# FFN fused values stored as interleaved high and low words: the down products read every second word as weights

## The chip, the cores and the metric

The kernel runs on one core of a Trainium2 chip. The metric is the device time of one execution in microseconds (us), taken as the median of several runs; lower is better. Every time below comes from those runs or from one profiled execution of the kernel.

## The reference

The input x has shape (4, 512, 512) in float32. Two blocks follow each other, each on a layer-normed input and each added back to it:

```python
# attention: 16 heads of 32
q, kv = (x @ W_q.T), (x @ W_kv.T)          # per head of 32
qf, kvf = fft(q), fft(kv)                  # each scaled to unit length over the head
qv = qf * cumsum(kvf, axis=1)              # running sum over the 512 positions
x = x + real(ifft(qv)) @ W_o.T             # (on layernorm(x))

# feed-forward (FFN), weights rounded to float8_e4m3fn first
gate = silu((x @ gate_w) * gate_scale)     # 512 -> 1536
up = (x @ up_w) * up_scale
fuse = gate * up
x = x + (fuse @ down_w) * down_scale       # 1536 -> 512 (on layernorm(x))
```

## The kernel before

The four batch entries have 512 positions each, in four chunks of 128. The kernel writes its instructions in an order fixed by hand; no scheduler moves them. Tiles come from pools: a tile with a `tag` takes the oldest of that tag's `bufs` buffers, and its first writer waits for the last user of what lay there.

The attention runs over the 16 chunks. For every chunk the running sum is a product of a triangle of ones (`tri_r`) with the key `kn`. The key is split into two tiles, `kh` (its value rounded to float32r by ScalarE) and `kl` (what is left, by VectorE). `running` multiplies both with `tri_r` and adds them up; here the halves are the moving operand. `k_scaled` takes one buffer of tag "kh" and one of tag "kl", each with three buffers.

The FFN runs over 48 steps, that is four batches (`b`) by twelve groups of 128 of the 1536 hidden values (`m`), with n = 12 b + m. Step n is `inner(n)`:

- 16 products of 512 columns (L525): `gu` for gate and for up, each over four blocks of the 512 inputs and over the high and low halves `yh`, `yl` of the normed input. The FFN weights `wg`, `wu` are here the stationary operand (lhsT, loaded into TensorE by LDWEIGHTS); the halves are the moving one.
- ScalarE's silu gives `g` (L536), VectorE multiplies into `f` (L538), ScalarE casts the high half `fh` (L546), VectorE subtracts to get the low half `fl` (L548). These two halves of one [128, 512] value again go into tags "kh" and "kl", the buffers of the attention's halves. For one step, n == STEPS - LATE = 44, they take two buffers of tag "qv".

`down(n)` then multiplies the halves with the down weights `wd`. Here the halves are the weights that TensorE loads: 128 of their 512 columns for each of the four chunks c, eight products for a step (L561):

```python
for c in cs:
    for v in fused[n]:                       # fh, then fl
        nc.tensor.matmul(
            pds[b][c][:, s],
            lhsT=v[:, c * P : (c + 1) * P],  # loaded as weights
            rhs=wd[:, m, s],                 # streamed
```

`down(n - 1)` stands behind `inner(n)` in the order of TensorE, so that the halves of step n - 1 are made while the 16 products of step n run. The quantisation of the later FFN weights still runs on VectorE and ScalarE during the first steps (`next_parts`). The last four steps (`LATE`) keep their down products for the end: they run chunk by chunk there, chunk 3 in two halves of 256 columns, so that the results of the first chunks leave while the last are computed. `scaled_out` (L575) and `added_out` (L579) finish a chunk and write it out.

Of the kernel before, what the change touches and what calls it, by code (L numbers as in the profile page):

```python
# [9 lines left out]
F32R = mybir.dt.float32r  # L10
# [5 lines left out]
P = 128  # L16
# [19 lines left out]
def tile_fft_attention_then_fp8_ffn(  # L36
# [39 lines left out]
    B, S, D = x.shape  # L76
# [10 lines left out]
    work = ctx.enter_context(tc.tile_pool(name="work", bufs=2))  # L87
# [242 lines left out]
    def nm(i):  # L330
        return "%d_%d" % chunks[i]
# [49 lines left out]
    def scaled(i, j, t):  # L381
        nc.vector.scalar_tensor_tensor(
            heads(t),
            heads(pqs[i][j]),
            st_x[i][1],
            rns[i, j].unsqueeze(2).to_broadcast([P, H, HD]),
            ALU.mult,
            ALU.mult,
        )

    def k_scaled(i):
        kn = work.tile([P, D], F32, tag="kn", name=f"kn_{nm(i)}", bufs=1)
        scaled(i, 1, kn)
        if i in carries:
            row = carries.pop(i)
            nc.vector.tensor_tensor(kn[:1, :], kn[:1, :], row, ALU.add)  # L396
        kh = work.tile([P, D], F32R, tag="kh", name=f"kh_{nm(i)}", bufs=3)
        kl = work.tile([P, D], F32R, tag="kl", name=f"kl_{nm(i)}", bufs=3)
        nc.scalar.copy(kh, kn)
        kns[i] = (kn, kh, kl)  # L400

# [78 lines left out]
    def y_mean(b, c):  # L480
        st_y[b, c] = mean(ys[b][:, c, :], f"f{b}_{c}")
# [36 lines left out]
    def inner(n, on_pe, on_act, between):  # L518
        b, m = divmod(n, MC)
        pgu = []  # L520
        for j, w in enumerate((wg, wu)):
            p = ps.tile([P, S], F32, tag="b", name=f"gu{j}_{b}_{m}")
            for k in range(KC):
                for v in (yhs[b], yls[b]):
                    nc.tensor.matmul(  # L525
                        p,
                        lhsT=w[:, k, m * P : (m + 1) * P],
                        rhs=v[:, k, :],
                        start=k == 0 and v is yhs[b],
                        stop=k == KC - 1 and v is yls[b],  # L530
                    )
            pgu.append(p)
            if j == 0:
                on_pe(n, 0)
        g = work.tile([P, S], F32, tag="tmp", name=f"g_{b}_{m}")
        nc.scalar.activation(g, pgu[0], AF.Silu, scale=gus[:, 0, m : m + 1])  # L536
        f = work.tile([P, S], F32, tag="qn", name=f"f_{b}_{m}")
        nc.vector.scalar_tensor_tensor(f, pgu[1], gus[:, 1, m : m + 1], g, ALU.mult, ALU.mult)  # L538
        on_act(n)
        if n == STEPS - LATE:  # L540
            fh = work.tile([P, S], F32R, tag="qv", name=f"fh_{b}_{m}")
            fl = work.tile([P, S], F32R, tag="qv", name=f"fl_{b}_{m}")
        else:
            fh = work.tile([P, S], F32R, tag="kh", name=f"fh_{b}_{m}", bufs=3)
            fl = work.tile([P, S], F32R, tag="kl", name=f"fl_{b}_{m}", bufs=3)
        nc.scalar.copy(fh, f)  # L546
        between(n)
        nc.vector.tensor_tensor(fl, f, fh.bitcast(F32), ALU.subtract)  # L548
        fused[n] = (fh, fl)
        on_pe(n, 1)  # L550
# [78 lines left out]
    summed(0, 0)  # L629
    norms(0, 0)  # L630
    k_scaled(0)
    k_low(0)

# [21 lines left out]
    x_mean(3)  # L655
    summed(1, 0)
    k_scaled(1)
    norms(1, 0)
    fold_out(wo, raw[2], 0)
# [33 lines left out]
    for i in range(3, N):  # L693
# [3 lines left out]
        if 0 <= i - (N - 9) < TC:  # L697
            load_y(0, [i - (N - 9)])
        spectrum(i, 1)
        k_scaled(i - 1)  # L700
        at(finish, i - 4)
        while wanted:
# [50 lines left out]
    def on_pe(n, part):  # L753
        if part == 1 and n == 0:
            running(N - 1)
            products(N - 1)
            combined(N - 1)
            v_out(N - 1)
            project(N - 3, "tp")
            load_unit(U1 + 2)  # L760
            load_unit(U1 + 3)
            v_back(N - 1)

    def on_act(n):
        b, m = divmod(n, MC)
        if b + 1 < B and 0 <= m - 3 < TC:
            y_mean(b + 1, m - 3)

    def between(n):
        if 0 < n < MC:  # L770
            next_parts(3 if n < 4 else 1)
# [30 lines left out]
    for n in range(STEPS):  # L802
        inner(n, on_pe, on_act, between)
        if 0 < n <= STEPS - LATE:
            b, m = divmod(n - 1, MC)
            down(n - 1, range(TC))
            if m == MC - 1:
                for c in range(TC):
                    scaled_out(b, c)
                    added_out(b, c, nc.gpsimd)  # L810
        behind(n)
# [3 lines left out]
    b = B - 1  # L815
# [83 lines left out]
```

## Time and profile before

| | |
|---|---|
| median of 3 runs | 460.06 us (459.68 to 460.41) |
| the profiled execution, whole | 460.13 us |
| its span in the profile | 458.3 us |
| mean granted clock of TensorE | 0.999 |
| PE (TensorE matmul) busy | 451.8 us, 1680 products |
| PEld (TensorE weight load) busy | 309.4 us, 1680 loads |
| DVE (VectorE) busy | 282.8 us |
| ACT (ScalarE) busy | 212.7 us |
| POOL (GpSimd) busy | 189.9 us |

The span is the stretch that the profiler sees; the 1.8 us between it and the whole time lie around it. PEld runs beside PE: the load of the next weights overlaps the product that runs. The duration of a record is not its share of time on TensorE, since products and loads are pipelined: 512-column products have records of 389 ns but start 227 ns after each other. The engines' names in the profile's rows are followed by the line of the kernel and by the tiles (output<-inputs); numbers of buffers are left out.

### The profile page before, as it was taken

Reading aid. Unit: us, or ns where it says so; the run is one execution under the profiler, and the core shown is the slowest. Engines: PE = TensorE matmul, PEld = TensorE weight load, DVE = VectorE, ACT = ScalarE, POOL = GpSimd, SP = SyncE. Lnnn points to the kernel's source line nnn. Section 1 sums busy time; section 2 is a strip of 40 time slices with the busy share of each in tenths; the row PEclk is TensorE's granted clock in tenths of the full one; section 3 lists DMA queues with packets and bytes.
Section 4 is the critical chain, followed back from the end, with each engine's and each line's share of the span. In section 5 each row is a group of like instructions: output and inputs, shape, how many; then the busy total and the mean of one; then the engine's idle time right before and its main releaser. Section 6 shows DMA issues by size and latency. Waiting matters only on the chain.

```text
span 458.3 us, 5074 instructions
## 1 busy us (share of the span) xinstructions
PE 451.8 (99%) x1680; PEld 309.4 (68%) x1680; DVE 282.8 (62%) x393; ACT 212.7 (46%) x430; POOL 189.9 (41%) x133
## 2 busy tenths in 40 slices
PE   9999999999999999999999999999999999999995
PEld 8544444444444445676888888888888888888884
DVE  1376999997999889798995432343533333532235
ACT  4468665556875632338934225433235432222220
POOL 0477897898897778510342230022401021400001
PEclk9999999999999999999999999999999999999999
DMA  8826356656678665752341050430131420200002
GB/s 301 296 78 190 99 162 161 183 148 186 196 205 210 172 142 162 206 156 81 92 93 23 0 185 23 93 69 1 48 138 39 98 48 1 92 1 0 0 1 92
DMA packets 91753, 51.22 MB, mean 112 GB/s; under 512 B 70608, under 2 KB 71248, under 8 KB 91728
## 3 DMA queue, kind: packets, MB, share of 16 engines
q1 hardware_dynamic: 91056, 50.75, 39.0%
q8 instruction: 13, 0.21, 0.2%
q10 hardware_dynamic: 672, 0.16, 0.2%
q14 instruction: 12, 0.10, 0.1%
HBM read 34.09 MB, written 16.78 MB: 111 GB/s over the span
## 4 chain that ended last, share of the span: by engine, by line
PE 82%; DVE 5%; ACT 4%; POOL 4%; issue 3%; DMA 2%; SPq 1%; DVEq 0%; ACTq 0%; POOLq 0%
PE gu L525 37%; PE pd L561 19%; PE pq L358 14%; PE po L457 7%; POOL rn L379 2%; DMA qv_all<-qv 1%; PE cum L413 1%; PE pkv L162 1%; ACT sq L369 1%; PE pw L162 1%; PE idle L592 1%; ACT qm L218 1%; DVE kn L396 1%; PE pwo L175 1%; ACT qa L217 1%
## 5 line engine op out<-in xcount | busy, mean ns | idle before, releaser
L379 POOL TENSOR_TENSOR rn<-ss,nhalf 128x16 f32<-128x16 f32 x32 | 103.6, 3237 | 12.6 <-DVE ss L374 12.4
L538 DVE SCALAR_TENSOR_TENSOR f<-gu,gus,g 128x512 f32<-128x512 f32 x48 | 36.0, 749 | 105.3 <-PE gu L525 101.7
L525 PE MATMUL gu<-yh,wg 128*128 128x512 f32 x192 | 76.6, 399 | 0.0
L561 PE MATMUL pd<-wd,fh 128*128 128x512 f32 (+1 forms) x196 | 75.1, 385 | 0.0
L561 PE MATMUL pd<-wd,fl 128*128 128x512 f32 (+1 forms) x196 | 75.0, 385 | 0.0
L525 PE MATMUL gu<-yh,wu 128*128 128x512 f32 x192 | 74.8, 390 | 0.0
L525 PE MATMUL gu<-yl,wg 128*128 128x512 f32 x192 | 74.7, 389 | 0.0
L525 PE MATMUL gu<-yl,wu 128*128 128x512 f32 x192 | 74.7, 389 | 0.0
L546 ACT CAST fh<-f 128x512 fp32r<-128x512 f32 x48 | 29.8, 621 | 81.9 <-DVE f L538 81.9
L536 ACT ACTIVATE g<-gu,gus 128x512 f32<-128x512 f32 x48 | 32.9, 686 | 53.3 <-PE gu L525 53.0
L358 PE MATMUL pq<-wq,xT 128*128 128x512 f32 x128 | 57.6, 593 | 0.0
L358 PE MATMUL pq<-wkv,xT 128*128 128x512 f32 x128 | 57.5, 592 | 0.0
L457 PE MATMUL po<-wo,qvT 128*128 128x512 f32 x128 | 57.5, 592 | 0.0
L548 DVE TENSOR_TENSOR fl<-f,fh 128x512 fp32r<-128x512 f32 x48 | 35.7, 744 | 27.5 <-ACT fh L546 27.5
L579 POOL TENSOR_TENSOR o<-o,ys 128x512 f32<-128x512 f32 x13 | 16.4, 1294 | 79.0 <-DVE o L575 70.1
L358 PEld LDWEIGHTS pq<-wkv,xT 128*128 128x128 f32 x128 | 24.2, 190 | 30.1 <-issue 28.5
L297 POOL TENSOR_TENSOR dev_f<-dev_f,nhalf 128x1 f32<-128x1 f32 x16 | 12.3, 768 | 72.9 <-ACT dev_f L296 72.7
L525 PEld LDWEIGHTS gu<-yh,wg 128*128 128x128 f32 x192 | 36.0, 188 | 8.9 <-issue 0.7
L561 PEld LDWEIGHTS pd<-wd,fh 128*128 128x128 f32 x196 | 36.8, 188 | 7.4
L561 PEld LDWEIGHTS pd<-wd,fl 128*128 128x128 f32 x196 | 36.8, 188 | 7.4
L358 PEld LDWEIGHTS pq<-wq,xT 128*128 128x128 f32 x128 | 23.2, 190 | 27.4 <-issue 27.0
L525 PEld LDWEIGHTS gu<-yl,wg 128*128 128x128 f32 x192 | 36.0, 188 | 8.2 <-issue 1.0
(88 smaller groups left out, 612.1 us busy)
## 6 DMA issues: line engine op xcount, KB each, us to landing
x<-in_x SPq DMA_DIRECT2D x16, 256.0 KB, 3.4
xT<-in_xT SPq DMA_DIRECT2D x16, 256.0 KB, 3.1
qv_all<-qv SPq DMA_DIRECT2D x16, 256.0 KB, 4.1
zv<-qv_all SPq DMA_DIRECT2D x64, 64.0 KB, 2.6
y_all<-x SPq DMA_DIRECT2D x16, 256.0 KB, 2.8
ys<-y_all SPq DMA_DIRECT2D x16, 256.0 KB, 3.8
xn_all<-xn_f SPq DMA_DIRECT2D x16, 256.0 KB, 2.5
z<-xn_all SPq DMA_DIRECT2D x64, 64.0 KB, 2.6
```

What stands on the lines that cost most here:

```text
L162: nc.tensor.matmul(pw[:, j * P : (j + 1) * P], lhsT=r[:, j, i * P : (i + 1) * P], rhs=fwd, start=True, stop=True,)
L297: nc.gpsimd.tensor_tensor(rstd, rstd, nhalf[:, 0:1], ALU.pow)
L358: nc.tensor.matmul(pq, lhsT=xTs[i][:, k, :], rhs=w[:, k, :], start=k == 0, stop=k == KC - 1)
L379: nc.gpsimd.tensor_tensor(rns[i, j], sss.pop((i, j)), nhalf, ALU.pow)
L457: nc.tensor.matmul(po, lhsT=qvT[:, k, :], rhs=wo[:, k, :], start=k == 0, stop=k == KC - 1)
L525: nc.tensor.matmul(p, lhsT=w[:, k, m * P : (m + 1) * P], rhs=v[:, k, :], start=k == 0 and v is yhs[b], stop=k == KC - 1 and v is yls[b],)
L536: nc.scalar.activation(g, pgu[0], AF.Silu, scale=gus[:, 0, m : m + 1])
L538: nc.vector.scalar_tensor_tensor(f, pgu[1], gus[:, 1, m : m + 1], g, ALU.mult, ALU.mult)
L546: nc.scalar.copy(fh, f)
L548: nc.vector.tensor_tensor(fl, f, fh.bitcast(F32), ALU.subtract)
L561: nc.tensor.matmul(pds[b][c][:, s], lhsT=v[:, c * P : (c + 1) * P], rhs=wd[:, m, s], start=m == 0 and v is fused[n][0], stop=m == MC - 1 a ...
L579: add.tensor_tensor(o, o, ys[b][:, c, s], ALU.add)
```

## The change

The two halves of a split value become one tile. For the attention's key it is `k2`, [128, 2, 512], with the high half in front and the low half behind it; each half is still contiguous. For the FFN's fused value it is `f2`, [128, 512, 2]: word 2j is the high half and word 2j + 1 the low half of value j. `fh` and `fl` become views of it with a step of two words. ScalarE's cast writes with this step, VectorE's subtraction reads and writes with it, and every load of weights for a down product reads 128 words with it. Both tiles use one tag, "kk", of three buffers, each as large as a "kh" and a "kl" buffer together. Step 44's tile takes a buffer of the tag "qa", which the quantisation has left by then.

```diff
@@ k_scaled
-        kh = work.tile([P, D], F32R, tag="kh", name=f"kh_{nm(i)}", bufs=3)
-        kl = work.tile([P, D], F32R, tag="kl", name=f"kl_{nm(i)}", bufs=3)
+        k2 = work.tile([P, 2, D], F32R, tag="kk", name=f"k2_{nm(i)}", bufs=3)
+        kh, kl = k2[:, 0, :], k2[:, 1, :]
@@ inner
         if n == STEPS - LATE:
-            fh = work.tile([P, S], F32R, tag="qv", name=f"fh_{b}_{m}")
-            fl = work.tile([P, S], F32R, tag="qv", name=f"fl_{b}_{m}")
+            f2 = work.tile([P, S, 2], F32R, tag="qa", name=f"f2_{b}_{m}")
         else:
-            fh = work.tile([P, S], F32R, tag="kh", name=f"fh_{b}_{m}", bufs=3)
-            fl = work.tile([P, S], F32R, tag="kl", name=f"fl_{b}_{m}", bufs=3)
+            f2 = work.tile([P, S, 2], F32R, tag="kk", name=f"f2_{b}_{m}", bufs=3)
+        fh, fl = f2[:, :, 0], f2[:, :, 1]
```

No instruction is added, removed or moved: on each engine the built program has the same instructions in the same order with the same waits. What differs is the addresses and the step of the operands named above.

## Prediction

> **What bounds the kernel now.** I read the chain of waits first, because it says which engine an added nanosecond has to be on. From about 184 us on it is TensorE alone, step after step, without a gap: 16 gate and up products, then eight down products.
>
> ```profile
> PE 82%; DVE 5%; ACT 4%; POOL 4%; issue 3%; DMA 2%; SPq 1%; DVEq 0%; ACTq 0%; POOLq 0%
> ```
>
> The same chain in order of time, near its end (start, length, engine, line, how many):
>
> ```profile
> 424.37 3.63 PE gu L525 x16
> 427.99 1.81 PE pd L561 x8
> 429.81 3.63 PE gu L525 x16
> 433.43 1.81 PE pd L561 x8
> 435.25 10.88 PE gu L525 x48
> 446.13 7.36 PE pd L561 x40
> ```
>
> The reader is to see that the FFN's time is a count of products times their beat: 1.81/8 and 3.63/16 are both 227 ns, whether the weights are `fh`/`fl` or `wg`/`wu`. So whatever the changed loads do matters only if it lengthens this beat, or starves TensorE of its halves.
>
> The groups of instructions, kept apart by shape, give the loads and the two engines that write the halves:
>
> ```profile
> L561 PEld LDWEIGHTS pd<-wd,fh 128*128 128x128 f32 x196 | 36.8, 188 | 7.4
> L561 PEld LDWEIGHTS pd<-wd,fl 128*128 128x128 f32 x196 | 36.8, 188 | 7.4
> L548 DVE TENSOR_TENSOR fl<-f,fh 128x512 fp32r<-128x512 f32 x48 | 35.7, 744 | 27.5 <-ACT fh L546 27.5
> L546 ACT CAST fh<-f 128x512 fp32r<-128x512 f32 x48 | 29.8, 621 | 81.9 <-DVE f L538 81.9
> L346 PEld LDWEIGHTS row<-tab,less 128*128 128x128 f32 x16 | 2.2, 137 | 3.8 <-issue 2.9 <-ACT wo L176 0.7 <-ACT kh L399 0.2
> ```
>
> 392 loads change, 188 ns each; ACT and DVE sit idle for tens of us before their part. The last row is a load whose 128 columns are one and the same word (step 0): 137 ns. It is a transpose as well, so it shows only weakly that the time of a load hangs on its step.
>
> The timeline of the end shows what a load costs when it does not fit behind a wide product. Columns: start, length, engine, instruction.
>
> ```profile
> 447.67 0.69 DVE L548 TENSOR_TENSOR fl<-f,fh 128x512 fp32r<-128x512 f32 x1 [0.69 <-ACT fh L546]
> ...
> 448.69 0.19 PEld L561 LDWEIGHTS pd<-wd,fl 128*128 128x128 f32 x1
> ...
> 452.00 0.28 PE L561 MATMUL pd<-wd,fl 128*128 128x256 f32 x1
> 452.00 0.19 PEld L561 LDWEIGHTS pd<-wd,fh 128*128 128x128 f32 x1
> 452.12 0.28 PE L561 MATMUL pd<-wd,fh 128*128 128x256 f32 x1
> 452.12 0.19 PEld L561 LDWEIGHTS pd<-wd,fl 128*128 128x128 f32 x1
> ```
>
> Products of 256 columns start 120 ns apart, each with a load of its own. So a contiguous load holds the load path for at most 120 of its 188 ns; the rest is latency that overlaps. At full width 227 - 120 = 107 ns of each beat are free for a slower load. In the 16 half-width products at the very end (2 halves x 4 steps x 2) nothing is known to be free. Early in the span the 128-column products are closer together still:
>
> ```profile
> 9.56 0.99 PEld L162 LDWEIGHTS pw<-tab,raw 128*128 128x128 f32 x8
> ```
>
> Eight loads in 0.99 us, 0.19 the last one: (0.99 - 0.19)/7 = 114 ns a load. I take 114 ns as what a contiguous load holds; it is a bound from above.
>
> **The loads.** 392 loads read 128 words spread over 256. No row of the trace has a load with step two. Below: no cost, or a gain (rival three). [...] The nearest rows are steps 0 and 1, 137 and 188 ns: 51 ns more for one more step, so a third step would be 239 ns, or 114 + 51 = 165 ns held. Holding in proportion to the words spanned gives 2 x 114 = 228 ns. I take the doubling: the step-0 row is a transpose and its slope is weak, and the words spanned are what the tile doubles. Then
> - 376 full-width products: 228 against a beat of 227, hidden: 0 us within the rounding. Were the true hold 120 ns, it would be 376 x (240 - 227) = 4.9 us.
> - 16 half-width products: 16 x (228 - 120) = 1.7 us, all on the path, for the last `scaled_out` halves start only when the last product ends (DVE was 0.29 us idle for it). With 165 ns held it would be 0.7 us.
>
> [...]
>
> **The halves' writers.** ScalarE's cast (621 ns) and VectorE's subtraction (median 691 ns) now write with step two. Below: nothing, as the FFT's strided pieces on VectorE (240 elements in runs of 15 with gaps) take 402 ns where a contiguous 128x256 product takes 421. Above: as if all 1024 words were passed, for which the rows are 1048 ns on ACT (L217) and 1330 ns on DVE (L254): +0.43 and +0.64 us. The runs of those FFT pieces are long, mine have one word, so I take half: +0.21 and +0.32 us. In most steps this is covered: `fl` ends at 430.23 (429.54 + 0.69) and is first loaded after 433 us, about 3 us later. The cover is thin in two places. In step 1 VectorE is late with quantisation; `fl` ends at 197.44 and its load starts at 197.54: 0.32 - 0.10 = 0.22 us of stall. At the end `fl` of the last step ends at 448.36 and is loaded at 448.69: 0.21 + 0.32 - 0.33 = 0.20 us. Together 0.4 us; from 0 to (0.64 - 0.10) + (1.07 - 0.33) = 1.3 us.
>
> [...]
>
> **What is shared now.** `k2` and the tag "kk" join buffers that were released apart: a new writer waits for the later of two readers, but the low half's reader directly follows the high half's on TensorE, and every wait in the built program is the one it was. Queues, transfers and quantisation are not touched. 0 us. Step 44's buffer of tag "qa" was last read by quantisation at 242 us (L254), some 190 us before.
>
> **The sum.** 1.7 + 0.4 = +2.1 us. The profiled execution took 460.13 us (span 458.3, 1.8 around it), 0.07 above the median of 460.06, so it stands for the runs: 462.2 us.
>
> **Rivals.**
> 1. Nothing happens: the load reads step two as fast as step one and the writers do too. For it: idle time before both writers and 107 free ns a beat. Against it: 16 half-width beats and two thin places where small extras show. 460.1 us, up to 460.9 if only the writers slow down.
> 2. The loads set the beat at full width. It decides from 227 ns held, twice my 114, so the forecast stands at its edge. At 2.5 times (285 ns): 376 x 58 + 16 x 165 ns = 24.4 us, 485 us with the writers' 0.4. At four times (456 ns): 376 x 229 + 16 x 336 ns = 91 us, 552 us. For it: the load is the only thing that every product does, and I cannot bound it from above. Against it: a factor over 2 means that skipping a word costs more than reading it.
> 3. Faster. float32 products (two passes, L358) start 429 ns apart, 214.5 for a pass of 512 columns; float32r ones 227. Something of 12 ns goes on in each float32r product, and if it is the handover from a load, a load that reads differently could save it: 392 x 12 ns = 4.7 us, 455.4 us. It needs the 12 ns to hang on the load's addresses; against it, `gu` with other weights has the same 227.
> That the change does not do what it says is excluded: the built program's weight operands have a step of two.
>
> **How the numbers follow.** Forecast (loads stretched, but hidden at full width): 0.38, from 460.9 to 466 (4.9 + 16 x 120 ns, or less, without the writers' extremes). Rival 1: 0.29. Rival 2: 0.26, half of it below 485. Rival 3: 0.07. About 0.2% (0.9 us) is what a measurement of this kernel can tell from no change: faster 0.07, same 0.29, slower 0.38 + 0.26 = 0.64. The range goes from 459.5, the low side of rival 1, to 484, half of rival 2; some 0.13 above and 0.06 below are left out. By the forecast's own case alone it would be 460.9 to 466.
>
> **What would show it.** Right: full-width down products still 227 ns apart (1.81 us for eight), the half-width ones some 228 instead of 120, `fl` and `fh` between 1 and 2 times as long, waits of TensorE for `fl` once near 197 us and once near 448 us. Wrong: eight down products in more than 1.9 us (rival 2), half-width ones still at 120 ns (rival 1), fewer than 1.8 us (rival 3).

## The result, and the profile after

The changed kernel takes 462.91 us (461.93 to 463.89, 4 runs) against 460.04 us before: 1.0059 times as long, with a 95% interval of 1.0045 to 1.0073, or +2.9 us (2.1 to 3.4). The profiled execution of after is its shortest run, 461.93 us, with a span of 460.1.

The chain of waits after the change, in order of time (start, length, engine, line, how many), at the same place as before:

```profile
424.02 1.87 PE pd L561 x8
425.89 3.63 PE gu L525 x16
429.52 1.87 PE pd L561 x8
431.39 3.63 PE gu L525 x16
435.02 1.87 PE pd L561 x8
436.89 10.89 PE gu L525 x48
447.78 7.53 PE pd L561 x40
```

Eight down products take 1.87 us instead of 1.81, and the forty at the end 7.53 instead of 7.36. Gate and up products stand nearly as before, 3.63 us for sixteen. Start to start in the trace, a full-width down product (512 columns) takes 233.4 ns instead of 226.7. That is 6.7 ns x 376 = 2.5 us, spread evenly over the FFN. By the starts in the trace the sixteen products behind each eight take 7 ns more as well (3.634 against 3.627 us), some 0.3 us over 44 steps.

In the profiled execution the span grew by 1.8 us only, since the attention before the FFN happened to be 0.8 us shorter: the last running sum starts at 183.65 us there, against 184.46 before. From that sum to the end it is 2.6 us longer. Such a shift is within what the runs of one kernel differ by.

The groups of instructions after, kept apart by shape:

```profile
L561 PE MATMUL pd<-wd,f 128*128 128x512 f32 x376 | 95.0, 394 | 0.0
L561 PE MATMUL pd<-wd,f 128*128 128x256 f32 x16 | 2.1, 282 | 0.0
L561 PEld LDWEIGHTS pd<-wd,f 128*128 128x128 f32 x392 | 74.7, 193 | 15.0
L546 ACT CAST f<-f 128x512 fp32r<-128x512 f32 x48 | 31.5, 656 | 82.2 <-DVE f L538 82.2
L548 DVE TENSOR_TENSOR f<-f,f 128x512 fp32r<-128x512 f32 x48 | 35.7, 744 | 28.8 <-ACT f L546 28.8
```

A load's record is 193 ns instead of 188. The cast takes 656 instead of 621 ns; the subtraction has the same mean of 744 ns (its median goes from 691 to 696). And the sixteen half-width products at the very end, which carried most of the forecast, in the timeline:

```profile
453.22 2.07 PE L561 MATMUL pd<-wd,f 128*128 128x256 f32 x16
```

The last record is 0.28 us long, so they start (2.07 - 0.28)/15 = 0.119 us apart: 120 ns before, 119 after. The slower load is not seen where nothing was known to be free, and it is seen where 107 ns were.

### The profile page after: what moved, and what is told of

Same layout as the page of the kernel before. It is cut to its first block, busy times and chain, and to the rows that moved or that the text cites. A ratio compares the mean times of both kernels' runs of the same rounds, so it can differ in the third digit from the quotient of the medians.

```text
span 460.1 us, 5074 instructions
## 1 busy us (share of the span) xinstructions
PE 454.0 (99%) x1680; PEld 311.4 (68%) x1680; DVE 282.6 (61%) x393; ACT 214.4 (47%) x430; POOL 190.2 (41%) x133
## 4 chain that ended last, share of the span: by engine, by line
PE 97%; DVE 1%; ACT 0%; issue 0%; DVEq 0%; ACTq 0%
PE gu L525 37%; PE pq L358 24%; PE pd L561 19%; PE po L457 11%; PE cum L413 2%; PE pkv L162 1%; PE idle L592 1%; PE pw L162 1%; PE pwo L175 1%; PE row L346 0%; DVE o L579 0%; DVE o L575 0%; DVE wu L252 0%; ACT g L536 0%; DVE kn L396 0%
## 5 line engine op out<-in xcount | busy, mean ns | idle before, releaser
L561 PE MATMUL pd<-wd,f 128*128 128x512 f32 (+1 forms) x392 | 96.9, 390 | 0.0
L561 PEld LDWEIGHTS pd<-wd,f 128*128 128x128 f32 x392 | 74.7, 193 | 15.0
L546 ACT CAST f<-f 128x512 fp32r<-128x512 f32 x48 | 31.5, 656 | 82.2 <-DVE f L538 82.2
L358 PE MATMUL pq<-wq,xT 128*128 128x512 f32 x128 | 57.6, 592 | 0.0
L358 PE MATMUL pq<-wkv,xT 128*128 128x512 f32 x128 | 57.5, 592 | 0.0
L548 DVE TENSOR_TENSOR f<-f,f 128x512 fp32r<-128x512 f32 x48 | 35.7, 744 | 28.8 <-ACT f L546 28.8
L358 PEld LDWEIGHTS pq<-wkv,xT 128*128 128x128 f32 x128 | 24.2, 190 | 30.1 <-issue 28.5
L358 PEld LDWEIGHTS pq<-wq,xT 128*128 128x128 f32 x128 | 23.2, 190 | 27.3 <-issue 27.0
L525 PEld LDWEIGHTS gu<-yh,wu 128*128 128x128 f32 x192 | 36.0, 188 | 7.5
L525 PEld LDWEIGHTS gu<-yl,wu 128*128 128x128 f32 x192 | 36.0, 188 | 7.5
```

The costliest lines, as they stand in the source:

```text
L358: nc.tensor.matmul(pq, lhsT=xTs[i][:, k, :], rhs=w[:, k, :], start=k == 0, stop=k == KC - 1)
L525: nc.tensor.matmul(p, lhsT=w[:, k, m * P : (m + 1) * P], rhs=v[:, k, :], start=k == 0 and v is yhs[b], stop=k == KC - 1 and v is yls[b],)
L561: nc.tensor.matmul(pds[b][c][:, s], lhsT=v[:, c * P : (c + 1) * P], rhs=wd[:, m, s], start=m == 0 and v is fused[n][0], stop=m == MC - 1 a ...
```

## The experiments

### Which part of the change costs it

Three kernels take one part each: the joined tile, the step of the loads, the step of the writers. The joined tile alone:

```diff
-            f2 = work.tile([P, S, 2], F32R, tag="kk", ...)
-        fh, fl = f2[:, :, 0], f2[:, :, 1]
+            f2 = work.tile([P, 2, S], F32R, tag="kk", ...)
+        fh, fl = f2[:, 0, :], f2[:, 1, :]
```

> One tile for both halves, but each half contiguous in it: the tile and its tags are those of the change, the step is not. If the step is the cause: the time of before, 460.0 us, 227 ns a down product, load records of 188 ns. If the joined tile or its place in memory is the cause: 462.9 us.

Measured: 460.02 us against 460.14, 0.9998 times (0.9989 to 1.0007). The joined tile costs nothing.

The loads alone, in the kernel before:

```diff
-                    lhsT=v[:, c * P : (c + 1) * P],
+                    lhsT=v[:, c // 2 * 2 * P : (c // 2 + 1) * 2 * P]
+                        .rearrange("p (j t) -> p j t", t=2)[:, :, c % 2],
```

> The kernel before with its two tiles and contiguous writers; only the loads of the down products read every second word (the positions of a batch come out in another order). If the loads carry the cost alone: 462.5 to 463 us, 233 ns a full-width down product, 120 ns a half-width one, writers at 621 and 691 ns. If the interleaved writers carry part of it: nearer to 460 us by that part.

Measured: 462.57 us against 460.14, 1.0054 times (1.0041 to 1.0067), +2.4 us. The groups by shape:

```profile
L561 PE MATMUL pd<-wd,fh 128*128 128x512 f32 x188 | 74.1, 394 | 0.0
L561 PEld LDWEIGHTS pd<-wd,fh 128*128 128x128 f32 x196 | 37.9, 193 | 7.6
L546 ACT CAST fh<-f 128x512 fp32r<-128x512 f32 x48 | 29.8, 622 | 82.2 <-DVE f L538 82.2
```

Products and loads have the records of the changed kernel, and full-width down products are 233 ns apart, while the cast is back at 622 ns.

The writers alone:

```diff
         nc.vector.tensor_tensor(fl, f, fh.bitcast(F32), ALU.subtract)
-        fused[n] = (fh, fl)
+        flat = f2.rearrange("p s t -> p (s t)")
+        fused[n] = (flat[:, :S], flat[:, S:])
```

> The changed kernel with writers of step two, but the loads read 128 adjacent words of the interleaved tile (wrong words, same number). If the loads carry the cost alone: 460.0 us, 227 ns a down product, cast 652 ns. If writers with gaps cost something at the thin places: up to 460.5 us.

Measured: 460.20 us against 460.14, 0.9995 times (0.9985 to 1.0005).

```profile
L562 PEld LDWEIGHTS pd<-wd,f 128*128 128x128 f32 x392 | 72.5, 188 | 14.9 <-DVE f L548 0.2
L546 ACT CAST f<-f 128x512 fp32r<-128x512 f32 x48 | 31.4, 655 | 81.9 <-DVE f L538 81.9
```

The cast is 34 ns longer. The writers show at one place, near 197 us in step 1: the load queue waits 0.2 us for the subtraction (end of the first row), and in the chain the eight down products at 197.92 us take 1.91 us instead of 1.81, a loss of 0.1 us. In this kernel the first load of a step already reads low words, so part of that wait is of its own making; the changed kernel has no such wait. The time of the whole kernel does not tell it from nothing. So the loads carry the whole cost that can be measured, and 376 x 6.7 ns = 2.5 us is most of it.

### What a load with a step costs by itself

Groups of products alone on the chip, the step and the width varied:

```python
lhsT = w[:, at : at + P * step].rearrange("p (j t) -> p j t", t=step)[:, :, 0]
nc.tensor.matmul(o[n % 4][:, :width], lhsT=lhsT, rhs=m[:, :width], start=True, stop=True)
```

> Not the reference's computation: groups of 24 float32r products by themselves, nothing beside them, each with a load of its own weights; the groups differ in the step between the words of a load (0, 1, 2, 3, 4, 8, 12) and in the width of the product (512, 384, 256, 128 columns). What is read is the beat from one product to the next. Theory L (the load's reads take slots from the stream of the moving operand, the more the farther its words lie apart): at 512 columns 227 ns at step 1, 233 at step 2, more at steps 3 and 4 (about 247 at 4), and from some step on no more. Theory F (a fixed loss at the handover as soon as words are not adjacent): 233 ns at every step above 1, and 6 ns more at 256 columns too. Theory H (the load gets slower, but is hidden behind a wide product): 227 ns at every small step, and the narrow products, 120 ns at step 1, are the first to grow.

Measured, from the timeline of TensorE (start, length, group; 24 products each). `quart` is 128 columns wide, `half` 256, `full` 512; `one` to `twelve` is the step:

```profile
98.53 2.79 PE L108 MATMUL quartone<-mv,wr 128*128 128x128 f32 x24
101.16 3.02 PE L108 MATMUL quarttwo<-mv,wr 128*128 128x128 f32 x24
104.01 5.84 PE L108 MATMUL quartfour<-mv,wr 128*128 128x128 f32 x24
...
81.39 2.99 PE L108 MATMUL halfone<-mv,wr 128*128 128x256 f32 x24
84.22 3.04 PE L108 MATMUL halftwo<-mv,wr 128*128 128x256 f32 x24
87.10 5.78 PE L108 MATMUL halffour<-mv,wr 128*128 128x256 f32 x24
...
21.14 5.71 PE L108 MATMUL fullone<-mv,wr 128*128 128x512 f32 x24
26.68 5.72 PE L108 MATMUL fulltwo<-mv,wr 128*128 128x512 f32 x24
37.89 5.82 PE L108 MATMUL fullfour<-mv,wr 128*128 128x512 f32 x24
49.46 6.58 PE L108 MATMUL fulltwelve<-mv,wr 128*128 128x512 f32 x24
```

A beat is the row's length less the last record, over 23. At 128 columns it is what a load holds: (2.79 - 0.27)/23 = 110 ns at step 1, (3.02 - 0.28)/23 = 119 ns at step 2. At step 4 it is 235 ns by the starts in the trace, at step 8 242 (at 256 columns), at step 12 (at 512 columns) some 267. So step 2 slows the load by 9 ns, not by 110; the next doubling costs it another 116. The load is then no bound at 256 columns (118 and 120 ns) and far from one at 512.

None of the three theories got its number at 512 columns: 231 ns at step 1 as at step 2, where the kernel has 227 and 233. Theory H holds for the load itself, but the cost in the kernel had another condition.

### Where the load's words lie against the stream

In that table the loads started 8 words apart, in the kernel 128 words apart. The second table uses the kernel's starts beside others. In `kept` two products in a row write one bank, as in the kernel; in `rot` every product changes the bank:

> Not the reference's computation: groups of 32 float32r products by themselves. In the first such table full-width products stood 231 ns apart at steps 1 and 2 alike, not 227 and 233; there the starts of the loads went by 8 words, in the kernel they go by 128 words and two products in a row write one bank. Theory P (where the words of a load lie against the stream decides): with the kernel's starts 227 ns at step 1 and 233 at step 2, and the groups with one fixed start differ among themselves. Theory Q (the sum of two equal products on one bank, or the kernel's other engines, decide): the starts change nothing, 231 ns throughout; the groups with two products in a row on a bank differ from those that change the bank each time. Either way step 2 is told from step 1 by width: if the load's reads cost the stream something, the difference is there from the width at which the load is covered (320 to 512 columns); at 256 columns none, as in the changed kernel.

Measured, 32 products to a row:

```profile
24.93 7.42 PE L101 MATMUL keptone<-mv,wr 128*128 128x512 f32 x32
32.19 7.63 PE L101 MATMUL kepttwo<-mv,wr 128*128 128x512 f32 x32
...
54.38 7.56 PE L101 MATMUL eightsone<-mv,wr 128*128 128x512 f32 x32
...
143.31 6.65 PE L101 MATMUL widekeptone<-mv,wr 128*128 128x448 f32 x32
149.80 6.68 PE L101 MATMUL widekepttwo<-mv,wr 128*128 128x448 f32 x32
156.31 5.72 PE L101 MATMUL mostkeptone<-mv,wr 128*128 128x384 f32 x32
161.87 5.71 PE L101 MATMUL mostkepttwo<-mv,wr 128*128 128x384 f32 x32
```

With the kernel's starts the kernel's beats come back: (7.42 - 0.39)/31 = 227 ns at step 1 and (7.63 - 0.39)/31 = 234 at step 2, without any other engine at work. The banks do not matter: `rot` has the same 227 and 233 ns. Starts that go by 8 words give 231 at step 1. That is theory P. But the extra is there at 512 columns alone, and not from 320 on as expected: at 448 columns 203 ns for both steps, at 384 173, at 320 147, at 256 120. With these starts the beats that hold steady are whole multiples of 6.67 ns (18 for 120, 22, 26, 34 for 226.7, 35 for 233.3): full width at step 2 is one such unit later.

The third table scans single starts:

> Not the reference's computation: groups of 16 full-width products by themselves, each group with one fixed start of its loads (0 to 112 words at step 1, 0 to 96 at step 2) or of its moving operand. Seen so far: the beats that hold steady are all multiples of 6.67 ns (120, 147, 173, 227, 233: 18, 22, 26, 34 and 35), a product of w columns takes w/16 + 2 of them, and full width at step 2 takes one more; so do some starts at step 1. Theory Q (beats come in slots of 6.67 ns, and a load that is some ns late pushes a full-width product into the next one): steady groups at 227 or 233, 240 for a few, unsteady ones between; step 2 never under 233, or under it for a few starts. Theory R (the distance between the words of the load and those of the moving operand decides): moving both starts by the same number of words gives the 227 of start 0 back.

Measured, 16 products to a row; `oneaa`, `oneah`, `oneaq` are loads at step 1 that start at word 0, 12, 64; `movac` moves the streamed operand by 8 words; `botaa`, `botab`, `botac` move both, by 2, 4 and 8 words; `twoaa`, `twoao` are step 2 from word 0 and 64:

```profile
24.25 3.80 PE L101 MATMUL oneaa<-mv,wr 128*128 128x512 f32 x16
50.18 3.89 PE L101 MATMUL oneah<-mv,wr 128*128 128x512 f32 x16
83.68 3.79 PE L101 MATMUL oneaq<-mv,wr 128*128 128x512 f32 x16
105.86 3.90 PE L101 MATMUL movac<-mv,wr 128*128 128x512 f32 x16
128.00 3.86 PE L101 MATMUL botaa<-mv,wr 128*128 128x512 f32 x16
131.69 3.86 PE L101 MATMUL botab<-mv,wr 128*128 128x512 f32 x16
135.39 3.80 PE L101 MATMUL botac<-mv,wr 128*128 128x512 f32 x16
157.27 3.89 PE L101 MATMUL twoaa<-mv,wr 128*128 128x512 f32 x16
209.32 3.90 PE L101 MATMUL twoao<-mv,wr 128*128 128x512 f32 x16
```

At step 1, 227 ns come at starts 0 and 64; the 18 others in this table have 229 to 234. Moving the streamed operand by 8 words loses it (234), moving both by the same 8 words brings it back (227), and so do 16 to 128 words (227 to 229 by their rows). Moving both by 2 or by 4 words does not: both groups have 231. So theory R holds for moves by whole eights, and not for smaller ones: the distance between the two is not all that counts. Step 2 reaches 227 at none of the 16 starts; it has 230 to 234. Theory Q does not hold as put: seven of these 16 are at 230 to 232 by their rows and not at 233, and the 231 ns of `botab` is no multiple of 6.67. One more point does not fit a rule on starts alone: a start of 4 words held 227 in the second table, where it followed a group at 227, and 233 in the third, where it followed one at 233. So a beat also seems to depend on what went before.

### The same loss in the kernel without a step

The kernel before with its contiguous halves; only the starts of the loads move by 16 words:

```diff
-                    lhsT=v[:, c * P : (c + 1) * P],
+                    lhsT=v[:, (16, 144, 272, 336)[c] :][:, :P],
```

> The kernel before with contiguous halves in two tiles and step 1 everywhere; only the starts of the down products' loads move, from 0, 128, 256, 384 words to 16, 144, 272, 336 (16 words more, counted in blocks of 64; some words are wrong, one chunk is read from another place). In the table of single products a contiguous load holds 227 ns only where its start and that of the moving operand agree in blocks of 64 words, and 233 ns where they differ by 16. If that is the same loss as the step's: 460.1 + 376 x 6.5 ns = 462.5 us without any step, and the narrow products at the end still at 120 ns. If the step itself is needed in the kernel: 460.1 us.

Measured: 463.64 us against 460.37, 1.0067 times (1.0055 to 1.0080), +3.3 us. The chain:

```profile
433.08 3.65 PE gu L525 x16
436.74 1.86 PE pd L561 x8
438.60 10.91 PE gu L525 x48
449.51 7.50 PE pd L561 x40
```

Eight down products take 1.86 us with contiguous loads of 188 ns; the half-width ones stand 118 ns apart. No step is needed for the loss, nor a slower load. It cost 0.9 us more than expected, because the sixteen gate and up products behind it went from 3.63 to 3.65 us, 0.02 us in each of 44 steps; why they did is not shown. The beats of these down products are not steady (0.23 and 0.24 us from start to start in the timeline). A second form of this kernel, with the halves 16 words into longer tiles, has no time: the pool of these tiles needs 84 kb of a partition where 81 are left.

### A step of four

```diff
-                    lhsT=v[:, c * P : (c + 1) * P],
+                    lhsT=v.rearrange("p (j t) -> p j t", t=4)[:, :, c],
```

> The kernel before with its two tiles; the loads of the down products read every fourth word (positions come out in another order). In the table of single products a load of step 4 holds 234 ns at every width up to 384 and 235 at 512, against 119 for step 2. If that holds here: 376 x (235 - 227) = 3.0 us and 16 x (234 - 120) = 1.8 us, 464.9 us in all, so only 2.0 us above step 2, and the narrow products at the end at 234 ns. If instead the cost grows with the words spanned (6.5 ns for the second word, 13 more for the next two): 376 x 20 = 7.5 us, 467.5 us or more.

Measured: 465.33 us against 460.39, 1.0110 times (1.0093 to 1.0126), +4.9 us. Start to start 235.1 ns at full width, and the last products, half as wide:

```profile
456.31 0.39 PE L561 MATMUL pd<-wd,fh 128*128 128x256 f32 x1
456.54 0.39 PE L561 MATMUL pd<-wd,fl 128*128 128x256 f32 x1
456.78 0.39 PE L561 MATMUL pd<-wd,fh 128*128 128x256 f32 x1
```

They stand 233 ns apart, the full-width ones 235, and the first table has 235 at 128 columns: here the load itself is the bound, at either width. 376 x 8.4 ns + 16 x 113 ns = 3.2 + 1.8 = 5.0 us is the measured gap. This is the term that I had given to step 2.

### The loss doubled

The gate and up products instead of the down products:

```diff
-                        lhsT=w[:, k, m * P : (m + 1) * P],
+                        lhsT=w[:, k, m // 2 * 2 * P : (m // 2 + 1) * 2 * P]
+                            .rearrange("p (j t) -> p j t", t=2)[:, :, m % 2],
```

> The kernel before; instead of the down products, the 768 gate and up products load every second word (of two neighbouring groups of 128, so the columns come out in another order). If each full-width product loses one slot of 6.67 ns whatever tile it loads from: 460.1 + 768 x 6.67 ns = 465.2 us, eight down products at 1.81 us and sixteen gate and up products at 3.73 instead of 3.63 us. If the loss belongs to the halves' own tiles (written shortly before, on the same buffers): 460.1 us.

Measured: 472.23 us against 460.37, 1.0253 times (1.0239 to 1.0267), +11.9 us, 6.8 more than expected. The chain, then TensorE's waits and two products behind the longest of them:

```profile
441.46 3.73 PE gu L525 x16
445.19 1.82 PE pd L561 x8
```

```profile
PE gu L525 <- DVE wg L252: 3.3, 2, 3.1
PE gu L525 <- DVE wu L252: 1.5, 1, 1.5
```

```profile
217.37 0.63 PE L525 MATMUL gu<-yl,wg 128*128 128x512 f32 x1
217.80 0.63 PE L525 MATMUL gu<-yh,wu 128*128 128x512 f32 x1
```

Sixteen products take 3.73 us, as expected, 233.4 ns each: 768 x 6.7 = 5.1 us. Of the rest, 3.3 + 1.5 = 4.8 us are waits for weights that are still being quantised, which the kernel before does not have: the load with a step spans the columns of two groups, and the built program waits for them earlier. Behind the longest wait products start 427 ns apart: by their starts, nine take 3.76 us from 216.91 us on, where nine at 233.4 ns would take 2.10, an estimated 1.7 us more. So the loss per full-width product is the same from another tile; nearly all of the rest is of this experiment's making.

## Why the prediction was right, point by point

The direction and the size were right (+2.1 us forecast, +2.9 measured, within the range), but by terms that changed places, and that is luck: 2.1 us that did not come stand against at least 2.5 us that the sum put at nothing. By the prediction's own signs it was not right. It asked for 1.81 us for eight down products and 228 ns for half-width ones; measured are 1.87 us and 119 ns. (Its upper bound of 466 us for the forecast's own case does not follow either: 460.1 + 4.9 + 1.9 is 466.9.)

- **"Holding in proportion to the words spanned gives 2 x 114 = 228 ns."** The hold of a load at step 2 is 119 ns, against 110 at step 1. The 114 ns was a fair bound; the doubling was not there. It comes at step 4 (235 ns). My reason, that the tile doubles the words spanned, was worth less than the slope that I set aside, 51 ns for a step; that was too high as well. The first table has loads at step 0 too: their records are 190 ns (`fullzero`), as at step 1, so the 137 ns of that row do not come with the step alone.
- **"16 half-width products: 1.7 us."** Measured 0: 120 and 119 ns.
- **"376 full-width products: hidden, 0 us."** This is the step that failed. I took the free 107 ns of each beat for cover, as if a load could cost a product only by ending late. It ended in time (119 ns held of a beat of 227), and the product still started 6.7 ns later: 2.5 us, nearly the whole result. What a load and a streamed operand do to each other while both run was not in the sum. The trace of before held a hint: 227 ns for 512 columns of float32r is 12 ns more than half of the 429 ns of a float32 record. That half a record is a pass of 512 columns was my estimate; at the second table's slope of 26.7 ns for 64 columns, 512 columns take 213 ns. (A float32 product is two such records, with two loads: L358 has 256 of each in the trace for the program's 128 products. What the prediction calls a product there is one of them, and the 1680 products of the profile before are records too.) I used it only for rival three.
- **The halves' writers, 0.4 us.** Too high. The cast grew by 35 of the 210 ns that I took, the subtraction by 5 of 320. Neither thin place opened: in the profile after, TensorE has no wait in the FFN for `fl`.
- **The joined tile, 0 us.** Right (`pair_contiguous`, 0.9998).
- **Rival 1** (nothing) was right on the writers, nearly right on the load's own rate (119 ns against 110), and wrong on the beat. **Rival 2** was right that all 376 products pay, and wrong in its mechanism and its price: it needs the load as the bound, which even step 4 gives only by 8 ns a product. **Rival 3** is out: no group at step 2 and 512 columns had a shorter beat than the 227 ns of the kernel before.

Shown by the runs: the loads alone carry the cost; it is 6.7 ns for each product of 512 columns; it does not need a step; it depends on where the load's words lie against the streamed operand's, though not on the distance alone. What delays the product is not shown. The 227 ns at starts 0 and 64, and their return when both are moved by 8 words or more, speak for the place of the words; that 2 or 4 words for both do not bring them back (231 ns), and that nothing is lost at 320 to 448 columns (147, 173 and 203 ns at both steps), where the load is covered as well, do not follow from it. Open: why the extra is there at 512 columns and not at 448 or less.

## What to carry to other kernels

Time hidden behind a product need not be free (here a load at step 2 cost 6.7 ns for each float32r product of 512 columns, and nothing at 256 to 448): cost a slower or moved load by the start-to-start time of the products around it, at their own width, and not by whether it ends in time. Float32r halves used as weights did best here contiguous (227 ns against 233 at step 2), with each load starting at the same place in a block of 64 words (256 bytes) as the operand streamed against it: the third table has 227 ns at starts 0 and 64 and 229 to 234 at the 18 others, though a start of 4 words had 227 in the second. Counted from the starts of their tiles, both kernels' 227 ns products have that. No version tried beats the kernel before: a joined tile with contiguous halves equals it (0.9998 times).

## What was not expected of the hardware

- In these tables a streamed operand is far more sensitive to a step than a load. In the first table a full-width product with a contiguous load but every second word streamed (`mover`) has a beat of (11.04 - 0.64)/23 = 452 ns, twice the contiguous one:

```profile
122.11 11.04 PE L108 MATMUL mover<-mv,wr 128*128 128x512 f32 x24
```

- Float32 products did not mind the step of the load at all: their records stand 429 ns apart at steps 1, 2 and 4, though the load's record goes from 191 to 308 ns. The loss was seen in float32r products of full width only.
- With the kernel's starts the beats of float32r products at step 1 are whole multiples of 6.67 ns, the time of 16 columns at their slope of 26.7 ns for 64: w/16 + 2 of them for a product of w columns, at 256, 320, 384 and 512; at 512 and step 2 it is one more. That is no rule for every case: 448 columns have 203 ns and not 200, and other starts have beats from 227 to 234.
